# A hybrid transformer block on one core: second sequence's local attention in the rotary part's buffers, and four smaller edits

## Chip, core and metric

The kernel runs on one core of a Trainium2 chip. The metric is device time in microseconds of one execution; lower is better. "PE" is TensorE, "DVE" VectorE, "ACT" ScalarE, "POOL" GpSimd and "SP" SyncE.

## What is computed

The input `x` holds 16 sequences of 512 tokens and 256 channels, all in fp32. Four residual stages follow each other; each normalizes its input (layer norm without weights) and adds its result to `x`:

```python
x = x + _L0_attn_a_ref(_layernorm(x), Wq, bq, Wk, bk, Wv, bv, Wo, bo)   # local attention, 16 heads of 16
x = x + _L0_ffn_ref(_layernorm(x), w_gate, w_up, w_down)                # silu(gate) * up, hidden 768
x = x + _L0_attn_b_ref(_layernorm(x), Wqkv, Wout, bout)                 # rotary attention, 16 heads of 16
x = x + _L0_ffn_ref(_layernorm(x), w_gate, w_up, w_down)                # the same weights again
```

Stage a masks the scores: a token sees its 32 neighbours on either side, and the first four tokens see and are seen by all. Stage b is unusual: its numerator is `exp` of the scores of rotated queries and keys under a causal mask, while its denominator is the sum of `exp` of the unrotated scores over all keys. The feed-forward weights are integers times 1/127.

## The kernel before

One sequence is the unit of work: 512 tokens are four tiles of 128. The stages are called `a`, `f`, `b` and `h` in names and lines (`psc_gf` is a gate product of the first feed-forward part, `psc_gh` of the second). Every stage is a Python generator that yields operations with an estimated cost, the results it needs and the buffers it takes. A planner, `Plan.run`, simulates the five engines with these estimates at build time, chooses the operation that could start first on its engine, and emits it; the order in which instructions stand on each engine is the order in which the planner emitted them. So cost estimates (`LAG`, `BORDER`), the wanted distances between stages (`LEAD`, in sequences) and the numbers of buffers (`Plan({...})`) decide the order. On the chip each engine runs its list in order and waits on semaphores.

PE works in three forms, which the planner calls `lying`: the full array (`FULL`); four row strips of 32, one per head pair, for scores (`ROWS`: `sa` L664, `dn` L1097, `nm` L1157); and four column strips, for values (`COLS`: `ya` L834, `yb` L1217, `og` L929, `gq` L884). It has eight PSUM banks; a row-strip block takes four of them.

The steps of a sequence, with the names that the profile shows:

- Layer norm (`normalize`): per tile `bn_stats` and `bn_aggr` (L419, L420), then `rstd` on POOL (L424, L425), four subtract-and-multiply on DVE (`xn`, L429), transposes on PE (`lt_a`, `lt_f`, `lt_b`, `lt_h`, L457), and copies to `xnt` on DVE (L465) and ACT (L467). All of it begins when the last tile of the stage before is added.
- Local attention: `psc_ka` and `psc_qa` (L537), `psv_a` (L515), key and query copies, and splits of the queries by head parity (`split_heads`, L552: a product with a mask of one number per partition). Scores `sa`, mask added on DVE (L694), then for each half of the heads: maximum (L707, DVE), subtraction (L709, POOL), exponential (L716, ACT), sum (L718, DVE), product with the reciprocal (L724, POOL). The result is transposed (`tp`, L778), copied (`pt`, L783 on DVE and L785 on ACT), and multiplied with values (`ya`, L834) in two pieces per tile, each waiting for two of the four `pt`. Values shifted by half a block (`vw`) come by DMA from `va`. The four global tokens go their own way (`sgp`, `gq`, `tg`, `og`, `pgp`, L849). `project_out` (L491, `po_a`) ends a tile and DVE adds it to `x` (L497).
- Feed-forward: six pairs `psc_g*`, `psc_u*`, tanh on ACT (L959), two products on DVE (L961, L967), and `po_f` or `po_h`.
- Rotary attention: `psc_qb`, `psc_kb`, `psv_b`; the denominators' scores `dn` with 64 exponentials that sum (L1078); rotated scores `nm` with exponentials into a buffer `ptb` (two of them) and a causal select on POOL (L1133), values `yb`, reciprocals transposed (`dbp`, L1186), and `po_b`.

The local part's queries, keys and values of one sequence are in single buffers (`qa`, `kp`, `va`, behind the locks "a" and "va"), the rotary part's in `qb`, `qr`, `kt`, `kr` and `vb` (locks "b", "br" and "vb"). Stages of different sequences run beside each other: while sequence n is in `b`, sequence n+1 or n+2 is in `a`. At the start there is only sequence 0, at the end only sequence 15.

Of the kernel before, what the change touches and what calls it, by code (L numbers as in the profile page):

```python
# [15 lines left out]
P = 128  # L16
S = 512
# [38 lines left out]

# [9 lines left out]

def pe(us, *needs, **how):
    return Op("pe", us, *needs, **how)

# [4 lines left out]

def dve(n, *needs, us=0.0, **how):
    return Op("dve", us or 0.07 + 0.00105 * n, *needs, **how)

# [4 lines left out]

LAG = {"pe": 0.26, "act": 0.17, "dve": 0.17, "pool": 0.15, "sp": 0.1}
BORDER = 0.2
NEVER = 1e9


class Plan:
# [3 lines left out]
    def __init__(self, slots):  # L92
        self.free = dict.fromkeys(LAG, 0.0)
        self.at = {}
        self.slots = {tag: [0.0] * n for tag, n in slots.items()}
        self.threads = []
        self.lying = FULL
        self.done = {}
# [42 lines left out]

    def run(self):
        while True:
# [17 lines left out]
            if engine == "pe":  # L161
# [4 lines left out]
                        self.lying != FULL and c[1][1].lying != self.lying,  # L166
                        self.progress(c[1]),
                    ),
                )
            else:  # L170
                start, t = min(soon, key=lambda c: (not c[1][1].gives, c[1][4], c[0]))
            op = t[1]
            us = op.us
            if engine == "pe":
                if op.lying != self.lying:
                    us += BORDER
                self.lying = op.lying
                key = t[2], t[3]
# [13 lines left out]
LEAD = {"a": 0.0, "f": 0.962, "b": 2.002, "h": 2.847}  # L192
SHARE = {"a": 44.0, "f": 33.0, "b": 66.0, "h": 33.0}


@with_exitstack
def kernel(
# [108 lines left out]
    kp = const.tile([P, NC, KP], F32, tag="kp", name="kp")  # L306
    mask3 = const.tile([P, 3, P], F32, tag="mask3", name="mask3")
    sign = const.tile([P, 1], F32, tag="sign", name="sign")

    def zeros():  # L310

        yield pool(0, us=0.6, makes="zeros")
        nc.gpsimd.memset(kp[:, :, 0:HALF], 0.0)
        nc.gpsimd.memset(kp[:, :, HALF + S :], 0.0)
# [3 lines left out]
        nc.gpsimd.memset(va[:, :, :, 1, :], 0.0)  # L318

# [16 lines left out]
        yield pool(0, 30.0, us=0.5, makes="zeros_b")  # L336
        nc.gpsimd.memset(vb[:, :, :, 1, :], 0.0)
# [14 lines left out]
    def values_bias():  # L352
# [3 lines left out]
        for kc in range(NC):  # L356
# [20 lines left out]
            "pt": 3,  # L377
# [31 lines left out]
    def normalize(stage, b):  # L409

        me = f"{stage}{b}"
        needs = added(before[stage], b) if stage in before else [f"x{b}"]
        slot = input_of[stage]
        op = yield dve(0, *needs, us=1.8, takes=("xn", slot))
        xt = xs[b]
        stats = work.tile([P, NT, 6], F32, tag="stats", name=f"stats_{me}")
        mv = work.tile([P, NT, 2], F32, tag="mv", name=f"mv_{me}")
        for t in range(NT):
            nc.vector.bn_stats(stats[:, t, :], xt[:, t, :])  # L419
            nc.vector.bn_aggr(mv[:, t, :], stats[:, t, :])  # L420
        k_xn, k_in = op.k["xn"], op.k[slot]
        op = yield pool(0, op.end, us=1.3)
        rstd = work.tile([P, NT], F32, tag="rstd", name=f"rstd_{me}")
        nc.gpsimd.tensor_scalar(rstd, mv[:, :, 1], EPS, None, ALU.add)  # L424
        nc.gpsimd.tensor_tensor(rstd, rstd, neg_half, ALU.pow)  # L425
        op = yield dve(0, op.end, us=1.35)
# [48 lines left out]
        "a": ["wa", "zeros", "zeros_a"],  # L475
# [74 lines left out]
    def split_heads(dst, src, oc, par):  # L550

        nc.vector.tensor_scalar(dst[:, par, oc, :], src, par_mask[:, par : par + 1], None, ALU.mult)  # L552

    def window_attention(b):
# [4 lines left out]

        tiles = {}  # L560
# [3 lines left out]
        def query(ps, oc, k, at):  # L564
# [5 lines left out]
            for par in range(2):  # L570
                op = yield dve(0, op.end - 0.17 if par else op.end, us=0.4)
# [3 lines left out]
        for oc in range(NC):  # L575
            op = yield pe(1.72, *fed(me), takes=("u",) if oc else ("u", "a"))
            if oc == 0:
                tiles["qa"] = work.tile([P, 2, NC, S], F32, tag="qa", name=f"qa_{b}")
            ps = channels(op, xnt[me], wk_sb, oc * P, f"ka{b}_{oc}")

            def key(_, oc=oc, ps=ps):
                nc.scalar.activation(
                    kp[:, oc, HALF : HALF + S], ps, AF.Identity, bias=bqk_sb[:, 1, oc : oc + 1]
# [7 lines left out]
        yield from values("a", b, va, wv_sb, 0, "va", (("in_a", 0),))  # L591

        def copies():
            op = yield Op("sp", 0.3, *(f"v_{me}.{t}" for t in range(NT)), takes=("vw",))
            nc.sync.dma_start(vw[0][HALF:P], va[0 : P - HALF])
            nc.sync.dma_start(vw[0][0:HALF, 1:NT], va[P - HALF : P, 0 : NT - 1])
            nc.sync.dma_start(vw[1][0 : P - HALF], va[HALF:P])
            nc.sync.dma_start(vw[1][P - HALF : P, 0 : NT - 1], va[0:HALF, 1:NT])
# [9 lines left out]
        for oc in range(NC):  # L608
            for dst, src in ((kg, kp[:, oc, HALF : HALF + NG]), (qg, q[oc][:, 0:NG])):
# [34 lines left out]
        go(global_queries(b, qg))  # L644
        go(global_values(b))
        go(weighted(b))

        for t in range(NT):
# [3 lines left out]
                f"qa_{me}.1",  # L652
# [728 lines left out]
```

## Time and profile before

| what | us |
|---|---|
| median of 3 runs | 2685.93 (2683.07 to 2686.07) |
| the profiled execution | 2689.26 |
| its span, first to last instruction | 2687.5 |
| PE busy | 2610.2 (97%) |
| DVE busy | 1573.4 (59%) |
| ACT busy | 1461.5 (54%) |
| POOL busy | 958.3 (36%) |
| mean granted PE clock | 0.988 |

A profiled execution records every instruction with its start and end. "Busy" is the time in which at least one instruction of an engine ran; matmuls are pipelined, and their ends are modelled, so a busy PE need not be at its peak. A line of the page or of an answer names the source line, the engine, the operation, `out<-in`, the count, and then busy and mean times or the idle time before it with what ended it. The clock is the share of full speed that PE was granted.

### The profile page before, as it was taken

What the parts mean: (1) busy time and instruction counts of PE and PEld (TensorE: products, weight loads), DVE (VectorE), ACT (ScalarE), POOL (GpSimd) and SP (SyncE); (2) the same over time, 40 slices, a digit from 0 to 9 for tenths busy, and PEclk for the clock granted to TensorE, in tenths of its full rate; (3) what the DMA queues carried; (4) which work ended last, traced back from release to release, by engine and by line L of the source; (5) the groups of instructions that cost most, each with busy time, mean ns of one, the idle gap of its engine ahead of it and who ended that gap; (6) DMA issues with size and microseconds to landing.
All of it is one profiled execution on the core that took longest, in us unless ns stands there. A gap on an engine that the chain in (4) does not pass through costs nothing.

```text
span 2687.5 us, 55762 instructions
## 1 busy us (share of the span) xinstructions
PE 2610.2 (97%) x23396; PEld 1494.5 (56%) x23396; DVE 1573.4 (59%) x3062; ACT 1461.5 (54%) x3553; POOL 958.3 (36%) x965
## 2 busy tenths in 40 slices
PE   5899999999999999999999999999999999999997
PEld 3555556455565655656455565655656465564544
DVE  6775755566565655746566565656746566563412
ACT  2337474554746556374554746556474554746462
POOL 4543525153341523425153341523425153250301
PEclk8899999999999999999999999999999999999999
DMA  4000010000100000010000100000010000100000
GB/s 134 24 1 23 2 39 2 23 17 1 39 2 23 17 23 17 1 39 2 23 17 1 39 2 23 17 23 17 2 39 1 23 17 1 31 2 9 1 8 8
DMA packets 26586, 49.31 MB, mean 18 GB/s; under 512 B 2336, under 2 KB 21216, under 8 KB 26336
## 3 DMA queue, kind: packets, MB, share of 16 engines
q1 hardware_dynamic: 24976, 44.83, 5.8%
q8 instruction: 183, 3.00, 0.5%
q10 hardware_dynamic: 1360, 0.93, 0.1%
q14 instruction: 67, 0.55, 0.1%
HBM read 13.77 MB, written 8.39 MB: 8 GB/s over the span
## 4 chain that ended last, share of the span: by engine, by line
PE 88%; DVE 9%; POOL 2%; ACT 1%; issue 1%; DMA 0%; ACTq 0%; POOLq 0%; DVEq 0%
PE dn L1097 10%; PE po_h L491 7%; PE psc_gh L537 7%; PE psc_gf L537 6%; PE psc_uh L537 6%; PE nm L1157 6%; PE psc_uf L537 6%; PE po_f L491 6%; PE yb L1217 6%; PE tp L778 4%; PE sa L664 3%; PE psv_b L515 2%; PE psv_a L515 2%; PE ya L834 2%; PE psc_ka L537 2%; PE po_b L491 2%
## 5 line engine op out<-in xcount | busy, mean ns | idle before, releaser
L1078 ACT ACTIVATE dn<-dn 128x512 f32<-128x512 f32 x1024 | 597.1, 583 | 132.4 <-PE dn L1097 129.5
L1124 ACT ACTIVATE ptb<-nm 128x512 f32<-128x512 f32 x640 | 330.2, 604 | 230.4 <-PE nm L1157 230.0
L709 POOL TENSOR_TENSOR sc<-sc,sm 128x1056 f32<-128x1056 f32 x128 | 247.2, 1952 | 333.1 <-DVE sm L707 326.9
L1097 PE MATMUL dn<-kt,qb 32*128 32x512 f32 x2048 | 287.5, 636 | 0.0
L724 POOL TENSOR_TENSOR sc<-sc,sm 128x1056 f32<-128x1056 f32 x128 | 248.3, 1955 | 101.0 <-DVE sm L719 87.6
L1133 POOL TENSOR_SCALAR_AFFINE_SELECT ptb<-ptb 128x512 f32<-128x512 f32 x256 | 159.2, 642 | 301.5 <-ACT ptb L1124 301.5
L694 DVE TENSOR_TENSOR sc<-sa,mask 128x512 f32<-128x512 f32 x256 | 160.1, 683 | 77.9 <-PE sa L664 76.8
L537 PE MATMUL psc_gh<-xnt_h,wg_sb 128*128 128x512 f32 x384 | 186.2, 607 | 7.4 <-DVE xnt_h L465 7.3
L1157 PE MATMUL nm<-qr,kr 32*128 32x512 f32 (+3 forms) x2048 | 191.0, 465 | 0.3 <-ACT ptb L1124 0.3
L1078 ACT ACTIVATION_READ_ACCUMULATOR dn<-dn 128x1 f32 x1024 | 191.0, 187 | 0.0
L537 PE MATMUL psc_gf<-xnt_f,wg_sb 128*128 128x512 f32 x384 | 186.2, 608 | 0.6 <-DVE xnt_f L465 0.6
L537 PE MATMUL psc_uh<-xnt_h,wu_sb 128*128 128x512 f32 x384 | 185.1, 604 | 0.0
L537 PE MATMUL psc_uf<-xnt_f,wu_sb 128*128 128x512 f32 x384 | 183.6, 601 | 0.0
L718 DVE TENSOR_REDUCE sm<-sc 128x8 f32<-128x1056 f32 x128 | 158.5, 1238 | 41.2 <-ACT sc L716 41.0
L491 PE MATMUL po_h<-wd_sb,ht_h 128*128 128x256 f32 x768 | 182.0, 387 | 0.0
L491 PE MATMUL po_f<-wd_sb,ht_f 128*128 128x256 f32 x768 | 177.5, 381 | 0.6 <-ACT ptb L1124 0.5
L1217 PE MATMUL yb<-ptb,vb 128*32 128x512 f32 (+3 forms) x2048 | 168.0, 444 | 6.6 <-POOL ptb L1133 6.6
L491 PEld LDWEIGHTS po_h<-wd_sb,ht_h 128*128 128x128 f32 x768 | 141.0, 190 | 55.1 <-issue 12.6
L716 ACT ACTIVATE sc<-sc 128x1056 f32<-128x1056 f32 x128 | 136.5, 1092 | 58.5 <-POOL sc L709 58.5
L424 POOL TENSOR_SCALAR rstd_f<-mv_f 128x4 f32<-128x4 f32 x16 | 3.7, 230 | 456.1 <-DVE mv_f L420 456.1
L1097 PEld LDWEIGHTS dn<-kt,qb 32*128 32x128 f32 x2048 | 90.0, 184 | 119.4 <-issue 56.2
L707 DVE TENSOR_REDUCE sm<-sc 128x8 f32<-128x1056 f32 x128 | 155.1, 1241 | 0.0
(163 smaller groups left out, 4254.6 us busy)
## 6 DMA issues: line engine op xcount, KB each, us to landing
vw<-va SPq DMA_DIRECT2D x32, 576.0 KB, 5.7
x<-in_x_dram SPq DMA_DIRECT2D x16, 512.0 KB, 4.0
out_dram<-x SPq DMA_DIRECT2D x16, 512.0 KB, 2.9
vw<-va SPq DMA_DIRECT2D x32, 144.0 KB, 5.1
raw_wg_sb<-in_w_gate_dram SPq DMA_DIRECT2D x1, 768.0 KB, 9.7
raw_wu_sb<-in_w_up_dram SPq DMA_DIRECT2D x1, 768.0 KB, 11.1
raw_wd_sb<-in_w_down_dram SPq DMA_DIRECT2D x1, 768.0 KB, 10.9
wqkv_sb<-in_wqkv_dram SPq DMA_DIRECT2D x1, 768.0 KB, 11.6
```

The lines of the kernel that those rows point to most:

```text
L491: nc.tensor.matmul(po[:, :D], y_of(c), w_sb[:, c, :], start=(c == 0), stop=(c == n - 1))
L537: nc.tensor.matmul(ps, w_sb[:, kc, lo : lo + P], x_in[:, kc, :], start=(kc == 0), stop=(kc == NC - 1))
L694: nc.vector.tensor_tensor(flat[:, 4 * j : 4 * j + 4, 0:P], ps[j].rearrange("p c two w -> p (c two) w"), mask.unsqueeze(1).to_broadcast([P, ...
L709: nc.gpsimd.tensor_tensor(part, part, small[:, 0, hs].unsqueeze(2).to_broadcast([P, H // 2, P + NG]), ALU.add,)
L718: nc.vector.tensor_reduce(small[:, 1, hs], part, AX.X, ALU.add)
L724: nc.gpsimd.tensor_tensor(part, part, small[:, 1, hs].unsqueeze(2).to_broadcast([P, H // 2, P + NG]), ALU.mult,)
L1078: nc.scalar.activation(ps[j], ps[j], AF.Exp, scale=SCALE, accum_out=den[:, t, h : h + 1])
L1097: nc.tensor.matmul(ps[j], tiles["qb"][rows, par, oc, t * P : (t + 1) * P], tiles["kt"][rows, oc, :], start=True, stop=True,)
L1124: nc.scalar.activation(pt[:, j, :], ps[j], AF.Exp, scale=SCALE)
L1133: nc.gpsimd.affine_select(out=pt[:, :, at : at + P], in_=pt[:, :, at : at + P], pattern=[[0, 4], [1, P]], compare_op=ALU.is_ge, fill=0.0, ...
L1157: nc.tensor.matmul(ps[j][:, at : at + n], tiles["kr"][rows, oc, c * P : (c + 1) * P], tiles["qr"][rows, par, oc, c * P :], start=True, sto ...
L1217: nc.tensor.matmul(y_ps[rows, c * P :], vb[:, c, 4 * oc + j, par : par + 2, :], pt[:, j, at : at + n], start=len(seen) == 1, stop=len(seen ...
```

## The change

1. Sequence 1's local attention no longer waits for sequence 0's buffers: it takes `qb` for its split queries, a tile in the place of `qr` for its keys (`kp_2`), and `vb` for its values, and starts as a thread of its own beside sequence 0. Its scores still come after sequence 0's. `vb`'s zeros are written early for that.
2. Layer-norm statistics are made per tile, each as soon as its tile is added; `stats`, `mv` and `rstd` have a buffer per stage.
3. `split_heads` becomes a product of two tensors, with the mask broadcast along the row.
4. The values `ya` of a tile are one piece that waits for all four `pt`; `pt` has four buffers for three.
5. In the last two sequences every other exponential tile of `nm` takes a buffer of the local part's scores (`sc`) instead of `ptb`.
6. The planner's estimates change: `LAG`, `BORDER`, `LEAD`, the choice among PE operations (a price `TURN` for another form, where form came before progress), the choice on the other engines (by progress), a slow stretch of PE after a pause of over 1.5 us, and single costs. `tg` now also waits for `vw`.

The matmuls are the same in number and shape, and so are the DMAs. The core of the diff:

```diff
-LAG = {"pe": 0.26, "act": 0.17, "dve": 0.17, "pool": 0.15, "sp": 0.1}
-BORDER = 0.2
+LAG = {"pe": 0.26, "act": 0.2, "dve": 0.2, "pool": 0.2, "sp": 0.1}
+BORDER = 0.19
...
+    def turn(self, lying):
+
+        if lying == self.lying:
+            return 0.0
+        return TURN["out"] if self.lying == FULL else TURN["in"] if lying == FULL else TURN["mid"]
...
                         c[1][4],
-                        self.lying != FULL and c[1][1].lying != self.lying,
-                        self.progress(c[1]),
+                        self.progress(c[1]) + self.turn(c[1][1].lying),
...
-                start, t = min(soon, key=lambda c: (not c[1][1].gives, c[1][4], c[0]))
+                start, t = min(soon, key=lambda c: (not c[1][1].gives, c[1][4], self.progress(c[1])))
...
+                if start - self.free[engine] > 1.5:
+                    self.slow = start + 4.2
+                if start < self.slow:
+                    us += min(us, (self.slow - start) / 2)
...
-LEAD = {"a": 0.0, "f": 0.962, "b": 2.002, "h": 2.847}
+TURN = {"out": 0.15, "mid": 0.02, "in": 0.3}
+LEAD = {"a": 0.0, "f": 0.796, "b": 1.467, "h": 2.654}
...
+    kp_2 = work.tile([P, NC, KP], F32, tag="qr", name="kp_2")
...
-            "pt": 3,
+            "pt": 4,
...
-        op = yield dve(0, *needs, us=1.8, takes=("xn", slot))
-        xt = xs[b]
-        stats = work.tile([P, NT, 6], F32, tag="stats", name=f"stats_{me}")
-        mv = work.tile([P, NT, 2], F32, tag="mv", name=f"mv_{me}")
         for t in range(NT):
+            op = yield dve(0, needs[t], us=0.51)
+            if t == 0:
+                xt = xs[b]
+                stats = work.tile([P, NT, 6], F32, tag=f"stats_{stage}", name=f"stats_{me}")
+                mv = work.tile([P, NT, 2], F32, tag=f"mv_{stage}", name=f"mv_{me}")
             nc.vector.bn_stats(stats[:, t, :], xt[:, t, :])
             nc.vector.bn_aggr(mv[:, t, :], stats[:, t, :])
...
-        nc.vector.tensor_scalar(dst[:, par, oc, :], src, par_mask[:, par : par + 1], None, ALU.mult)
+        mask = par_mask[:, par : par + 1].to_broadcast([P, S])
+        nc.vector.tensor_tensor(dst[:, par, oc, :], src, mask, ALU.mult)
...
+        second = b == 1
+        keys, v_all, locks, v_lock = (kp_2, vb, ("b", "br"), "vb") if second else (kp, va, ("a",), "va")
...
+                f"scored_a{b - 1}",
                 takes=("s", "sc", "small"),
-                gives=(("a", 0),) if t == NT - 1 else (),
+                makes=f"scored_{me}" if t == NT - 1 else None,
+                gives=[(lock, 0) for lock in locks] if t == NT - 1 else (),
...
-            for ns in ((0, 1), (2, 3)):
+            for ns in (range(4),):
...
-        op = yield pe(0.4, op.end, takes=("u",), gives=(("tmp", k_gp),))
+        op = yield pe(0.4, op.end, f"vw_{me}", takes=("u",), gives=(("tmp", k_gp),))
...
+        def home(i):
+
+            return "sc" if b >= B - 2 and i % 2 else "ptb"
...
-        plan.start(in_turn(bodies[stage], stage), stage, 0)
+        if stage == "a":
+            plan.start(bodies[stage](0), stage, 0)
+            plan.start(in_turn(bodies[stage], stage, 0, 1), stage, 1)
+        else:
+            plan.start(in_turn(bodies[stage], stage), stage, 0)
```

## The prediction

> **What bounds the kernel now.** I read the page first: its busy times, its 40 slices, and the chain that ended last.
>
> ```profile
> PE 2610.2 (97%) x23396; PEld 1494.5 (56%) x23396; DVE 1573.4 (59%) x3062; ACT 1461.5 (54%) x3553; POOL 958.3 (36%) x965
> ...
> PE   5899999999999999999999999999999999999997
> ...
> PEclk8899999999999999999999999999999999999999
> ...
> PE 88%; DVE 9%; POOL 2%; ACT 1%; issue 1%; DMA 0%; ACTq 0%; POOLq 0%; DVEq 0%
> ```
>
> TensorE (PE) works nearly all the time; only the first and last slices have holes. Next, busy time by stage (columns: width, then busy us of PE, PEld, DVE, ACT, POOL, then the granted clock):
>
> ```profile
> 0.00:60.00 60.00, 32.18 (x447) 21.93 (x447) 36.21 (x69) 12.39 (x18) 27.83 (x40) 0.83 0.48 150
> 60.00:120.00 60.00, 48.05 (x589) 31.18 (x587) 54.31 (x100) 19.38 (x31) 36.48 (x33) 0.89 0.10 26
> 120.00:300.00 180.00, 174.57 (x1874) 103.15 (x1876) 120.12 (x220) 97.34 (x230) 77.48 (x70) 0.97 0.04 10
> 300.00:2400.00 2100.00, 2088.16 (x19112) 1201.05 (x19105) 1261.32 (x2470) 1187.17 (x2892) 772.27 (x771) 1.00 0.06 17
> 2400.00:2600.00 200.00, 195.35 (x998) 99.64 (x997) 83.84 (x169) 112.67 (x311) 32.04 (x35) 0.99 0.01 4
> 2600.00:2687.50 87.50, 71.90 (x400) 37.55 (x392) 17.63 (x36) 32.51 (x73) 12.16 (x19) 0.90 0.04 13
> ```
>
> PE is idle 27.8 + 12.0 + 5.4 us in the first 300 us, 11.8 us in the next 2100, 20.3 us after that. The granted clock is below 1 only at the two ends; there PE is slow as well as idle. PE's waits name the holes:
>
> ```profile
> PE tg L909 <- DVE gp L905: 13.9, 1, 13.9
> PE lt_a L457 <- DVE xn_a L429: 10.1, 2, 9.5
> PE lt_f L457 <- DVE xn_f L429: 9.3, 4, 6.9
> PE lt_h L457 <- DVE xn_h L429: 8.6, 4, 4.6
> PE psc_gh L537 <- DVE xnt_h L465: 7.3, 13, 0.8
> PE yb L1217 <- POOL ptb L1133: 6.6, 6, 1.9
> ```
>
> The first four are sequence 0's softmax, the first load, and layer norms; all but the fifth lie mostly in the ramps. A busy PE is not at its best either. The timeline late in the run (start, length) shows it:
>
> ```profile
> 2500.87 1.15 PE L1157 MATMUL nm<-qr,kr 32*128 32x384 f32 x16
> 2501.95 1.07 PE L1217 MATMUL yb<-ptb,vb 128*32 128x384 f32 x16
> 2502.95 2.86 PE L491 MATMUL po_f<-wd_sb,ht_f 128*128 128x256 f32 x12
> 2505.74 1.15 PE L1157 MATMUL nm<-qr,kr 32*128 32x256 f32 x16
> ```
>
> From start to start, `nm` costs 1.08 us, `yb` 1.00, `po_f` 2.79. Alone, 512 columns in two passes take 0.858 us (a `psc` pair repeats every 1.717), so these stream in 0.858, 0.858 and 2.573. The rest, 0.22, 0.14 and 0.21, is the price of going from one form of tile (row strips, column strips, full array) to another. With that the profiled span divides: 9.5 us to the first matmul; 2313.6 of streaming (144.6 a sequence); 247.8 of turns between blocks; 4.7 after the last matmul; and 111.9 of waits and slow clock, namely 55.9 before 300 us, 20.9 from 300 to 2400, 35.1 after. The change leaves the matmuls alone, so it can act on the turns and on the 111.9.
>
> **Turns.** I counted neighbours in the order of instructions of both programs and priced them by the mean of the same kind in this trace, waits left out. Leaving row strips costs 0.22, full to row 0.153, column to full 0.143, column to row 0.124, full to column 0.108, full to full 0.049. Row to full goes 294 to 277, row to column 117 to 174, full to row 324 to 397, column to full 135 to 167, column to row 87 to 54, full to column 105 to 47, full to full 1059 to 1044; the few others hardly move. One value piece per tile does halve the runs of `ya` (128 to 64), but the planner's new rule for turns lets `dn` stand in 247 runs where it stood in 217. The sum goes from 247.8 to 253.7: **+6 us** (+2 to +10, since some neighbours are new).
>
> **Start.** `tg` waits for sequence 0's global softmax while DVE and POOL work down the local one:
>
> ```profile
> 35.91 1.64 PE L457 MATMUL lt_a<-ident,xn_a 128*128 128x128 f32 x8 [0.58 <-DVE xn_a L429]
> 51.44 0.68 PE L909 MATMUL tg<-ident,gp 64*128 64x64 f32 x4 [13.89 <-DVE gp L905]
> ```
>
> In the new order sequence 1's `psc_ka`, `psc_qa`, `psv_a` (4 x 1.72 + 4 x 0.9 = 10.5 us) stand in this hole; before, they filled PE between 69 and 90 us. Sequence 0's chain hardly changes. Eight mask adds at 0.62 a piece and four maxima at 1.19 end on DVE at 45.6 (46.8 before), then three subtractions and two products on POOL at 1.95 make tile 0 ready at 51.8, and `tp` starts at 52 where it started at 54.4. Now the price: those fillers are gone later. By the same durations PE waits about 4 us after the projections, 2.5 for `ya`, 1.3 for `yag`, 4.7 before the third tile's `tp` (DVE also has sequence 1's four splits), 2.5 for `pgp`, 1 for the fourth `tp` and 6 for `lt_f0`, whose layer norm gains 1.6 us as three of its four statistics (0.53 each) are made early. That puts `psc_gf0` at 104.5 instead of 110.5. With PE's own work before it (61.2 us of streaming and turns, 60.5 before), 40.5 us of waits become 33.8. After it, sequence 1 is further on, and `lt_f1` has 5.7 us of PE work between its last `po_a` and itself; the 9 us lost there before (2.9 idle, and 184.7 to 191.5 at a clock of 0.50) should fall to 3. Against this, more pauses keep the clock low: the pause of about 2.7 us at 183 was followed by that stretch of half clock, the 13.9 us one by half clock from 38 to 58. Five pauses of 2.5 to 6 us at 0 to 2 us each, little where PE waits anyway: I take 1. Together 6.7 + 6.3 - 1: 55.9 becomes 44, **-12** (-20 to -4).
>
> [...]
>
> **Splits.** 192 instructions change form.
>
> ```profile
> L552 DVE TENSOR_SCALAR qa<-q,masks x64: 435/486/2170, 23.1 to 2277.6; 128x512 f32<-128x512 f32 x64
> ...
> L694 DVE TENSOR_TENSOR sc<-sa,mask x256: 671/681/693, 33.0 to 2382.6; 128x512 f32<-128x512 f32 x128
> ```
>
> The old form takes 0.48 alone but up to 2.17 beside POOL (at 76.0 two took 3.85 us while a POOL product ran). Products of two SBUF tensors (L1009, L1011) took 0.69 alone and at most 1.26. Old busy sum: 110.8 us. New: 192 x 0.62 to 0.69 = 119 to 132 us. DVE is busy 60% of the middle, so this is hidden at **0**; without that cover it would be 1.3 us a sequence. [...]
>
> **Middle.** A sequence takes 161.1 us here: 144.6 of streaming, 15.3 of turns, 1.2 of waits (`lt_h` behind `xn_h`, `psc_gh` behind `xnt_h`). Leads and lags change the order, so I compared the PE work between producer and consumer with the time from the one to the other in this trace. Last `po_b` to `lt_h`: 8.0 us of work becomes 10.3, the chain takes 8.0. `nm` to `yb`: 3.0 becomes 4.1, for 2.0 to 4.8. `tp` to `ya`: 1.7 becomes 2.2, for 0.7. Last `po_f` to `lt_b`: 8.6 becomes 7.0, for 7.5 less 1.6 of early statistics. `dn` to the next user of its banks: 2.1 becomes 2.0, for 1.9. Only `lt_h` to `psc_gh` shrinks to the bone: 3.1 becomes 1.9, for a copy of 0.69 and whatever DVE has queued. I take 0.5 us a sequence where there were 1.2, beside some 5 us in the first two sequences: 20.9 becomes 12, **-9** (-15 to +20).
>
> **Tail.** `lt_h14` cost about 5 us (2.6 idle, then 3.4 at half clock); it now has 7.7 us of `po_f` work ahead of it. The last rotary part, from `nm_15` at 2602.8 to `po_b15` at 2638.6, waits for two exponential buffers; with `sc` as a second pair ACT can run through: twelve exponentials at 0.6 from 2599.7, forty at 0.51, two copies, then 3.7 us of select, `yb` and product end at 2632 to 2636. The last layer norm saves 1.6. **-12** (-15 to -3).
>
> Vector memsets, DMA orders and the fourth `pt` buffer cost nothing: POOL is idle 1.5 us before the first `rstd`, and the counts of DMAs are equal.
>
> **Sum.** -12 - 9 - 12 + 6 = -27 us. The profiled execution took 2689.26 (span 2687.5 and 1.8 around it), 3.3 above the median of the runs. So 2662 for such an execution, and 2685.9 - 27 = **2659** as a median.
>
> **Rivals.** *The start only moves its waits* (0.20): DVE is busy 54.3 of 60 us from 60 to 120, more than PE, and gets sequence 1's work earlier; the 12 us are not won, 2671. For it: the five new pauses. Against: the hole of 13.9. *All ramps fill* (0.12): start 20 and tail 15, 2646 or less. *DVE becomes the bound between layer norm and `psc_gh`* (0.07), slower: splits and per-tile statistics queue ahead of the `xnt_h` copy, and PE has 1.9 us of cover where it had 3.1. Each us late is 16 us; it eats the 27 at 1.7 us a sequence, and at 2.5 the time is 2699. Against: the copy is ranked first, and DVE has 40% free. *The order brings nothing* (0.06): the turns and new waits pay back what the ramps give, 2685.
>
> **Chances.** Forecast 0.55 (2650 to 2668). The measurement can tell about 0.2%, 5.4 us. Forecast, filled ramps and moved waits are faster: 0.87; nothing 0.06; slower 0.07. The range runs from -45 (start 20, middle 15, tail 15, turns +5) to -3 (start 4, tail 7, middle +2, turns +6): 2641 to 2683.
>
> **What would show it.** Right: no `tg` wait of 13.9; `psc_gf0` near 104 to 108; a spacing of 160.9 to 161.5 us between sequences; `po_b15` to the end unchanged but for 1.6 us; turns up. Wrong: `psc_gh <- xnt_h` above 1 us on every sequence; `psc_gf0` at 110 or later; splits above 1 us in the mean.

## The result, and the profile after

The changed kernel took 2718.86 us (median of 5 runs, 2717.86 to 2729.53), beside 2685.93 (2680.71 to 2686.8, 5 runs) for the kernel before on the same chip: a ratio of 1.014, 95% interval 1.0117 to 1.0163. (Further on, brackets behind a time hold the same two: the ratio to the kernel before and its interval.) It is 33 us slower where 27 us faster were forecast. The profiled execution took 2718.34 (span 2716.6).

The page of after, its busy times and its chain that ended last:

```profile
PE 2622.4 (97%) x23396; PEld 1492.2 (55%) x23396; DVE 1659.2 (61%) x3062; ACT 1456.5 (54%) x3553; POOL 1010.6 (37%) x967
...
PE 81%; DVE 17%; POOL 1%; issue 1%; DMA 1%; ACT 0%; ACTq 0%; SPq 0%; POOLq 0%; DVEq 0%
```

DVE has as many instructions as before and 86 us more work; its share of the chain went from 9% to 17%. Busy time by stage, after (columns as in the prediction):

```profile
0.00:60.00 60.00, 40.97 (x344) 26.84 (x352) 44.67 (x92) 15.75 (x24) 32.21 (x45) 0.94 0.50 150
60.00:120.00 60.00, 45.40 (x734) 31.32 (x716) 53.61 (x91) 17.70 (x28) 40.28 (x36) 0.89 0.10 26
...
300.00:2400.00 2100.00, 2059.08 (x18484) 1160.74 (x18488) 1300.19 (x2408) 1161.31 (x2854) 791.28 (x744) 1.00 0.06 17
```

The hole of the first 60 us is smaller (PE busy 41.0 where it was 32.2). In the middle, from 300 to 2400 us, PE is idle 40.9 us where it was 11.8. The clock is nearly full there: it was granted at half for two stretches of 6.8 us (from 316.3 and from 1804.5), where in before it never was. PE's waits in after (total us, times, longest):

```profile
PE dn L1111 <- DVE pt L797: 18.1, 12, 1.8
PE tp L792 <- DVE vb L533: 16.9, 12, 1.5
PE lt_a L464 <- DVE xn_a L436: 14.5, 4, 9.5
PE pgp L820 <- POOL pq L814: 7.4, 5, 4.4
PE lt_f L464 <- DVE xn_f L436: 6.4, 2, 5.0
PE lt_h L464 <- DVE xn_h L436: 4.5, 2, 3.6
```

The 13.9 us of `tg` are gone, and `lt_f` and `lt_h` wait less, as expected. The first two rows are new: 12 sequences, each 1.5 us for `dn` and 1.4 for `tp`. The releasers are plain copies of 0.4 to 0.7 us, so the question is what DVE did ahead of them. The timeline of one sequence (start, length; DVE, then POOL, then PE) answers it:

```profile
1621.05 3.32 DVE L560 TENSOR_TENSOR qb<-tmpb,masks 128x512 f32<-128x512 f32 x2
...
1629.57 2.10 DVE L1023 TENSOR_TENSOR tmpb<-tmpb,sins 128x512 f32<-128x512 f32 x1
...
1632.38 0.42 DVE L533 COPY vb<-psv_b 128x256 f32<-128x256 f32 x1
1632.72 3.09 DVE L560 TENSOR_TENSOR qr<-tmpb,masks 128x512 f32<-128x512 f32 x2
...
1637.73 0.68 DVE L797 COPY pt<-tp 128x512 f32<-128x512 f32 x1
...
1619.52 4.30 POOL L723 TENSOR_TENSOR sc<-sc,sm 128x1056 f32<-128x1056 f32 x2 [4.35 <-DVE sm L721]
1626.55 4.58 POOL L738 TENSOR_TENSOR sc<-sc,sm 128x1056 f32<-128x1056 f32 x2 [1.04 <-DVE sm L733]
1631.85 1.74 POOL L1017 TENSOR_TENSOR kr<-kt,cos 128x512 f32<-128x512 f32 x1
1633.56 1.71 POOL L1017 TENSOR_TENSOR tmpb<-tmpb,cos 128x512 f32<-128x512 f32 x1
...
1632.86 1.09 PE L792 MATMUL tp<-ident,sc 128*128 128x128 f32 x8 [1.46 <-DVE vb L533]
1638.46 1.14 PE L1111 MATMUL dn<-kt,qb 32*128 32x512 f32 x8 [1.82 <-DVE pt L797]
```

Two `qb` splits take 3.32 us while POOL's softmax products of the next sequence run; a sine product takes 2.10 beside the second pair; then come `vb`, two `qr` splits of 3.09 beside POOL's cosine products, and `pt`. PE waits for `vb` and for `pt`. The groups of DVE in after (busy, mean ns) show the splits' price:

```profile
L560 DVE TENSOR_TENSOR qb<-tmpb,masks 128x512 f32<-128x512 f32 x64 | 80.9, 1284 | 1.7 <-ACT tmpb L1032 1.7
L560 DVE TENSOR_TENSOR qr<-tmpb,masks 128x512 f32<-128x512 f32 x64 | 63.3, 1008 | 0.1
L560 DVE TENSOR_TENSOR qa<-q,masks 128x512 f32<-128x512 f32 x64 | 44.1, 729 | 114.2 <-ACT q L579 114.2
```

In before the same groups, in the old form, were these:

```profile
L552 DVE TENSOR_SCALAR qa<-q,masks 128x512 f32<-128x512 f32 x64 | 47.1, 773 | 32.4 <-ACT q L568 32.4
L552 DVE TENSOR_SCALAR qb<-tmpb,masks 128x512 f32<-128x512 f32 x64 | 32.5, 541 | 10.1 <-ACT tmpb L1018 10.1
L552 DVE TENSOR_SCALAR qr<-tmpb,masks 128x512 f32<-128x512 f32 x64 | 31.2, 511 | 0.9
```

From here on "splits" is count times mean over the 192: 116.8 us before, 193.3 after. (The prediction's 110.8 is busy time, which counts overlapping instructions once.)

The table divides every profiled span as the prediction did: streaming is taken as 2313.6 us in all of them, turns are counted from the order at the prediction's prices, waits are what is left by stage, so they hold what a lower clock costs as well.

| kernel | us, median | turns | waits to 300 | 300 to 2400 | later | DVE busy | splits |
|---|---|---|---|---|---|---|---|
| before | 2685.93 | 247.8 | 55.9 | 20.9 | 35.1 | 1573 | 117 |
| after | 2718.86 | 253.4 | 52.3 | 58.9 | 24.3 | 1659 | 193 |
| splits_back | 2687.71 | 253.4 | 51.0 | 30.7 | 22.5 | 1617 | 151 |
| splits_alone | 2699.70 | 247.8 | 53.9 | 31.3 | 40.0 | 1609 | 155 |
| old_rules | 2674.81 | 242.6 | 57.5 | 20.7 | 23.5 | 1627 | 169 |
| old_rules_ts | 2658.84 | 243.5 | 53.8 | 12.9 | 19.7 | 1581 | 122 |
| pool_narrow | 2651.18 | 253.4 | 37.3 | 8.9 | 21.2 | 1576 | 149 |
| pool_busy | 2653.80 | 253.4 | 40.8 | 9.5 | 21.5 | 1595 | 153 |

### The profile page after: what moved, and what is told of

It is laid out like the page before. It is cut to its first block, busy times and chain, and to the rows that moved or that the text cites. A ratio compares the mean times of both kernels' runs of the same rounds, so it can differ in the third digit from the quotient of the medians.

```text
span 2716.6 us, 55822 instructions
## 1 busy us (share of the span) xinstructions
PE 2622.4 (97%) x23396; PEld 1492.2 (55%) x23396; DVE 1659.2 (61%) x3062; ACT 1456.5 (54%) x3553; POOL 1010.6 (37%) x967
## 4 chain that ended last, share of the span: by engine, by line
PE 81%; DVE 17%; POOL 1%; issue 1%; DMA 1%; ACT 0%; ACTq 0%; SPq 0%; POOLq 0%; DVEq 0%
PE dn L1111 9%; PE po_h L498 7%; PE psc_gf L544 6%; PE nm L1176 6%; PE psc_uf L544 6%; PE po_f L498 6%; PE yb L1236 6%; PE psc_uh L544 6%; PE psc_gh L544 5%; PE tp L792 3%; DVE qb L560 3%; PE psv_a L522 2%; PE po_b L498 2%; PE sa L678 2%; PE psc_qa L544 2%; PE ya L848 2%
## 5 line engine op out<-in xcount | busy, mean ns | idle before, releaser
L723 POOL TENSOR_TENSOR sc<-sc,sm 128x1056 f32<-128x1056 f32 x128 | 253.3, 1998 | 213.6 <-DVE sm L721 211.9
L1111 PE MATMUL dn<-kt,qb 32*128 32x512 f32 x2048 | 305.0, 640 | 21.0 <-DVE pt L797 18.1
L738 POOL TENSOR_TENSOR sc<-sc,sm 128x1056 f32<-128x1056 f32 x128 | 258.0, 2029 | 59.2 <-DVE sm L733 57.8
L708 DVE TENSOR_TENSOR sc<-sa,mask 128x512 f32<-128x512 f32 x256 | 160.9, 682 | 51.3 <-PE sa L678 51.3
L1176 PE MATMUL nm<-qr,kr 32*128 32x384 f32 (+3 forms) x2048 | 188.8, 464 | 0.9 <-issue 0.9
L732 DVE TENSOR_REDUCE sm<-sc 128x8 f32<-128x1056 f32 x128 | 157.7, 1232 | 37.3 <-ACT sc L730 37.3
L498 PEld LDWEIGHTS po_h<-wd_sb,ht_h 128*128 128x128 f32 x768 | 141.0, 190 | 41.8 <-ACT dn L1092 13.9
L792 PE MATMUL tp<-ident,sc 128*128 128x128 f32 x1024 | 142.5, 288 | 21.7 <-DVE vb L533 16.9
L975 DVE SCALAR_TENSOR_TENSOR th_f<-th_f,psc_gf 128x512 f32<-128x512 f32 x96 | 65.3, 680 | 150.0 <-ACT th_f L973 149.4
## 6 DMA issues: line engine op xcount, KB each, us to landing
raw_wu_sb<-in_w_up_dram SPq DMA_DIRECT2D x1, 768.0 KB, 10.3
```

Of the source, the lines that this page charges most:

```text
L498: nc.tensor.matmul(po[:, :D], y_of(c), w_sb[:, c, :], start=(c == 0), stop=(c == n - 1))
L708: nc.vector.tensor_tensor(flat[:, 4 * j : 4 * j + 4, 0:P], ps[j].rearrange("p c two w -> p (c two) w"), mask.unsqueeze(1).to_broadcast([P, ...
L723: nc.gpsimd.tensor_tensor(part, part, small[:, 0, hs].unsqueeze(2).to_broadcast([P, H // 2, P + NG]), ALU.add,)
L738: nc.gpsimd.tensor_tensor(part, part, small[:, 1, hs].unsqueeze(2).to_broadcast([P, H // 2, P + NG]), ALU.mult,)
L792: nc.tensor.transpose(ps[:, j, :], sc[:, j, oc, par, 0:P], ident)
L1111: nc.tensor.matmul(ps[j], tiles["qb"][rows, par, oc, t * P : (t + 1) * P], tiles["kt"][rows, oc, :], start=True, stop=True,)
```

## Experiments 1: the form of the split, or the order

**Theory FORM**: the tensor product (edit 3) stalls beside POOL, VectorE comes late, PE waits. **Rival ORDER**: the planner's new rules (edit 6) put the work there, whatever its form. Two runs change the form alone, two the rules. "Rules" are `LAG`, `BORDER`, `LEAD`, `TURN`, both choices and the slow stretch.

```diff
 # splits_back: after, one instruction
-        nc.vector.tensor_tensor(dst[:, par, oc, :], src, mask, ALU.mult)
+        nc.vector.tensor_scalar(dst[:, par, oc, :], src, par_mask[:, par : par + 1], None, ALU.mult)
```

> The kernel after, with the split into heads as a product with a per-partition scalar again; the order of instructions on every engine is that of after. Theory FORM (the tensor product with a broadcast mask reads two SBUF tensors and stalls beside POOL's products, so VectorE comes late with the copies vb and pt): the splits fall from 193 us of VectorE to about 120, PE's waits from 300 to 2400 us fall from 59 to 15 to 25, time 2675 to 2690. Theory ORDER (the planner's new leads, lags and choice put VectorE's rotary work beside POOL's softmax products and the consumers close behind; the form of the split hardly matters, since the old form stalls beside POOL as well): the waits stay at 45 to 59, time 2705 to 2719.

Measured 2687.71 (ratio to before 1.0009, 1.0000 to 1.0019): 31 us of the 33 are gone, in the same order of instructions. The waits of the middle halve. But the splits fall only to 151 us. Its groups show that the old form is slow in these places too:

```profile
L559 DVE TENSOR_SCALAR qb<-tmpb,masks 128x512 f32<-128x512 f32 x64 | 65.0, 1037 | 1.7 <-ACT tmpb L1031 1.7
L559 DVE TENSOR_SCALAR qr<-tmpb,masks 128x512 f32<-128x512 f32 x64 | 48.7, 781 | 0.1
```

The form costs 1284 - 1037 = 0.25, 0.23 and 0.19 us, about the difference of the two alone (0.68 and 0.48). The stall on top is nearly the same (`qb` 0.60 us in the tensor product and 0.56 in the old form, `qr` 0.33 and 0.30): FORM was right in time (its waits of 15 to 25 were 30.7) and wrong in mechanism.

```diff
 # splits_alone: before, one instruction
-        nc.vector.tensor_scalar(dst[:, par, oc, :], src, par_mask[:, par : par + 1], None, ALU.mult)
+        mask = par_mask[:, par : par + 1].to_broadcast([P, S])
+        nc.vector.tensor_tensor(dst[:, par, oc, :], src, mask, ALU.mult)
```

> The kernel before, with the split into heads as a tensor product and nothing else; the order of instructions is that of before. FORM: VectorE's time in the splits rises from 111 to 170 or more, PE's waits in the middle from 21 to 45 or more, time 2710 to 2725. ORDER: the splits cost 0.2 us more each (192 of them, 35 to 40 us of VectorE), hidden by its idle 40 per cent; time 2683 to 2692.

Measured 2699.70 (1.0053, 1.0038 to 1.0068), between the two. The splits cost 38 us more of VectorE, 0.2 each, and 14 of them reach the end. `lt_h <- xn_h` (8.6 to 12.7) and `psc_gh <- xnt_h` (7.3 to 11.5), waits that were there before, grow by 8 of the 14. The 155 us also answer the prediction's bound of 119 to 132: it fails in the old order already.

> The kernel after, with the planner's lags, leads, price of a turn, rule of choice and clock model of before. Counted from the order and priced as in the prediction, its turns cost 242.6 us where after has 253.4. FORM: the tensor products stay, VectorE's splits stay above 160 us, and only the turns are won: 2700 to 2712. ORDER: the waits of the middle go as well: 2655 to 2680.

Measured 2674.81 (0.9958, 0.9942 to 0.9975): faster than before, with the tensor product. Turns fall and the new waits of the middle go, as ORDER said, though the splits still cost 169 us, as FORM said.

> The kernel before, with only the planner's new lags, leads, price of a turn, rule of choice and clock model. Turns by count 257.7 us (before 247.8). FORM: the old form of the split keeps VectorE in time; only the turns are lost, less something at the ends: 2685 to 2698. ORDER: the waits of the middle come with the rules, 40 us or more: 2715 to 2735.

Measured 2829.05 (1.0533, 1.0517 to 1.0548), far beyond both: the middle waits 137 us, with the clock at half for 116.1 us of it; `dn` waits 32.5 for `vb`, in an order where the old form of `qb` takes 1.28 us in the mean.

> The kernel after, with the planner's rules of before and the split as a product with a scalar (cost in the plan 0.4 again): the second sequence's place, the statistics by tile, the one value piece and the second exponential pair remain. Its turns are 243.5 us by count. If the tensor product costs in this order what it cost in that of before (14 us): 2658 to 2664. If an order that keeps it from POOL makes it free: 2671 to 2678. With the start or tail worth nothing: 2680 or more.

Measured 2658.84 (0.9906, 0.9891 to 0.9921), 0.94% or some 25 us faster than before, and no kernel with the whole computation was faster. Of the three cases it is the first (2658 to 2664). So, with edits 1, 2, 4 and 5 in all four:

| | old form of split | tensor product |
|---|---|---|
| rules of before | 2658.84 | 2674.81 |
| new rules | 2687.71 | 2718.86 |

The form costs 16 or 31 us, the rules 29 or 44: each costs more beside the other, as when both take slack from one engine. (In the upper row the planned cost of a split changes with the form, so a few instructions move too.)

## Experiments 2: is it POOL that VectorE waits for

Every DVE instruction of 300 to 2400 us in the trace of after, sorted by the POOL instruction that overlaps it most, gives these means: `qb` 1.29 us beside the softmax products (49 of 52); `qr` 0.67 alone and 1.34 and 1.75 beside the cosine products; the sine product 0.68 alone, 2.10 beside a softmax product. But `sc <- sa,mask`, which reads PSUM, 0.68 alone and 0.69 beside one, and the maximum over `sc`, which reads one SBUF tensor, 1.24 and 1.24. `xn_h`, a tensor_scalar that also reads one, takes 0.40 alone and 1.80 beside a softmax product. So of these the products of two SBUF tensors and tensor_scalar lose time (0.6 to 1.4 us beside a softmax product), and the mask add, which reads PSUM, and the maximum do not. The loss looks like a block: the two `qb` splits of the timeline above end 0.55 us behind the second softmax product (1624.37 and 1623.82).

Three runs test whether the time is lost there.

```diff
 # pool_narrow: after, both POOL products of the local softmax (the other one likewise)
-                part,
-                part,
-                small[:, 0, hs].unsqueeze(2).to_broadcast([P, H // 2, P + NG]),
+                part[:, 0:1],
+                part[:, 0:1],
+                small[:, 0, hs.start : hs.start + 1].unsqueeze(2).to_broadcast([P, 1, P + NG]),
 # pool_busy: the same, and after each product
+            nc.gpsimd.memset(part[:, 2:], 0.0)
+            nc.gpsimd.memset(part[:, 2:], 0.0)
```

> The kernel after in its own order, but POOL's two products of the local softmax (add of the maximum, product with the reciprocal) are done on one head of eight in each half: 132 columns of 1056, so POOL is free 1.7 us earlier each time. It leaves out the shift and the normalization of the other seven heads. Theory SHARE (the tensor product on VectorE is slow because it runs while POOL's product runs): qb falls from 1.28 to about 0.70 us in the mean, qr, whose neighbour is POOL's product with cos, stays at 0.9 or more, the wait of tp for vb goes, time 2680 to 2700. Rival FORM IN ITSELF (in this order the tensor product is slow for another reason, such as ScalarE writing beside it): qb stays above 1.1 us, time 2705 to 2719.

> The kernel after in its own order; POOL's two products of the local softmax are done on one head of eight, as in pool_narrow (2651 us), and POOL then writes zeros over the last six heads twice, so that it is busy about 2.0 us as in after but for three quarters of that time reads nothing from SBUF. It leaves out the shift and the normalization of the other heads. Theory STALL (the loss is VectorE's stall beside POOL's products of two SBUF tensors): VectorE is free again, splits qb 0.75 to 0.90 us in the mean, time 2650 to 2670, near pool_narrow. Rival LATENCY (pool_narrow was fast because each step of the softmax chain came 1.6 us earlier, and the copies behind it with it): time 2700 to 2719, near after, although the splits are short. Rival WRITES (any work of POOL in SBUF stalls VectorE): qb stays above 1.1 us.

pool_narrow measured 2651.18 (0.9879, 0.9863 to 0.9895), better than either theory said, and pool_busy 2653.80 (0.9889, 0.9872 to 0.9905). In pool_busy POOL is as long at each step as in after, as its groups show:

```profile
L747 POOL MEMSET sc<- 128x792 f32 x128 | 97.4, 761 | 7.4
...
L746 POOL MEMSET sc<- 128x792 f32 x128 | 97.1, 759 | 0.0
...
L740 POOL TENSOR_TENSOR sc<-sc,sm 128x132 f32<-128x132 f32 x128 | 59.5, 465 | 39.6 <-DVE sm L735 38.0 <-DVE sc L702 0.2
```

and in after:

```profile
L738 POOL TENSOR_TENSOR sc<-sc,sm 128x1056 f32<-128x1056 f32 x128 | 258.0, 2029 | 59.2 <-DVE sm L733 57.8 <-ACT th_f L973 0.2 <-DVE sc L702 0.2
```

0.47 + 0.76 + 0.76 = 1.98 us, where the whole product took 2.03. Yet the time falls by 65 us, as much as DVE's busy time (1659.2 to 1594.7). For the splits LATENCY and WRITES fall; STALL stands. Beside the zeros `qb` takes 0.73 in the mean, beside the products of after 1.29. The splits `qb` and the middle of pool_busy:

```profile
L560 DVE TENSOR_TENSOR qb<-tmpb,masks 128x512 f32<-128x512 f32 x64 | 48.5, 778 | 1.8 <-ACT tmpb L1036 1.7
...
300.00:2400.00 2100.00, 2099.21 (x19072) 1189.76 (x19075) 1284.49 (x2474) 1180.99 (x2889) 781.34 (x1181) 1.00 0.06 17
```

PE is idle 0.8 us of 2100. In the order of after, with the tensor products and with POOL as busy, hardly anything is late once DVE does not stall beside the softmax products. The splits are not all of it: they sum to 153 us here and to 151 in splits_back, which is 34 us slower. The stalled sine product (2.10 to 0.70) and `xn_h` (1.80 to 0.92) are cured here too, and not there.

```diff
 # qb_psum: after; the bank is given back behind the second split
-                split_heads(tiles["qb"], qt, oc, par)
+                split_heads(tiles["qb"], ps, oc, par)
```

> The kernel after, with the split of the unrotated query reading the projection's PSUM bank instead of ScalarE's copy of it in SBUF; the bank is given back after the second split instead of after the copy, so the plan moves a little (turns by count 250.5 us, after 253.4), and the splits qb still stand between softmax reductions of the next sequence, beside POOL's 2 us products. Theory SHARE (only instructions of VectorE that read SBUF alone, as two tensors or as one in the fast form, stall beside a POOL product of two SBUF tensors; in the trace of after the products with a PSUM operand keep 0.68 us beside it): qb falls from 1.28 to 0.66 to 0.70 us, VectorE gets back 35 to 40 us, and the time falls to 2685 to 2705. Rival FORM IN ITSELF (slow beside anything): qb stays above 1 us. Rival BANK (the bank comes free later and PE waits for it): qb 0.68, time 2715 or more.

("The fast form" is the product with a scalar, read from SBUF: 0.48 us alone where the tensor product takes 0.68.)

```profile
L560 DVE TENSOR_TENSOR qb<-psc_qb,masks 128x512 f32<-128x512 f32 x64 | 40.3, 671 | 3.0 <-ACT tmpb L1032 3.0
```

The split is cured: 0.67 us in the mean where after has 1.28, and 46 of 52 still stand beside POOL's softmax products. The time falls by 10 us only: 2708.79 (1.0085, 1.0070 to 1.0100), 4 us above the range. The middle:

```profile
300.00:2400.00 2100.00, 2081.09 (x18517) 1174.48 (x18519) 1267.07 (x2413) 1168.13 (x2861) 773.99 (x748) 0.99 0.06 17
```

PE is idle 18.9 us there where after has 40.9, but the clock was granted at half for 30.7 us where after has 13.7. `dn` still waits 7.7 us for `pt` and 4.8 for `vb`. The plan moved, and now one `xn_b` of each sequence meets POOL's product (1.49 us in the mean, 0.40 alone). So the operand's place cures this instruction (1.28 to 0.67 us); what the kernel wins by that alone is not shown, since order and clock changed with it.

> The kernel of old_rules_ts (2659) with the split of the unrotated query reading PSUM, as in qb_psum. Its turns are 243.5 us by count, as there. The splits qb cost 0.64 us in the mean there, so little is to be won: STALL gives 10 us of VectorE less and 2653 to 2660. If the later release of the bank or the moved order costs more: 2665 or more.

Measured 2658.91 (0.9910, 0.9895 to 0.9924), equal to old_rules_ts. It does not tell what the stall of `qb` is worth in that order: the scalar form takes 0.74 us from PSUM, alone and beside POOL's cosine products, where it took 0.64 in the mean from SBUF, so DVE got no time back (busy 1580.0 us, 1581.2 in old_rules_ts).

## Experiments 3: which rule

```diff
 # leads_old: after, one line
-LEAD = {"a": 0.0, "f": 0.796, "b": 1.467, "h": 2.654}
+LEAD = {"a": 0.0, "f": 0.962, "b": 2.002, "h": 2.847}
```

> The kernel after, with one line of the planner back: LEAD of before (a 0, f 0.962, b 2.002, h 2.847). In its order the splits qb and qr of a sequence stand behind the next sequence's last pt copies, no longer among its softmax reductions; by count its turns cost 238.4 us (after 253.4). Theory PLACE (the new leads put VectorE's rotary products beside POOL's 2 us softmax products): the mean split falls from 1.0 to about 0.69 us, the waits of the middle from 59 to 15 to 25, time 2658 to 2678. Rival CLOSE (the new choice of PE's next step and the lags put consumers close behind producers, whatever the leads): the waits stay above 40 and only the turns are won, 2698 to 2710.

Measured 2716.84 (1.0123, 1.0108 to 1.0138): neither. PLACE is half right on the splits (`qb` and `qr` at a median of 0.68 us, but a mean of 0.87 over all splits, since part of them meet POOL's products) and wrong on the time. Turns fall by 15 us by count. PE waits 29.9 us for `xn_a`, of which 15.2 are in the middle, where after has none. The timeline of leads_old (DVE, POOL, PE):

```profile
1266.03 4.46 DVE L436 TENSOR_SCALAR xn_a<-x,mv_a,rstd_a 128x256 f32<-128x256 f32 x4
...
1265.43 1.95 POOL L723 TENSOR_TENSOR sc<-sc,sm 128x1056 f32<-128x1056 f32 x1
...
1267.99 1.98 POOL L723 TENSOR_TENSOR sc<-sc,sm 128x1056 f32<-128x1056 f32 x1
...
1270.18 1.69 PE L464 MATMUL lt_a<-ident,xn_a 128*128 128x128 f32 x6 [1.62 <-DVE xn_a L436]
```

Four `xn_a`, 0.40 us each alone, take 4.46 between two softmax products: the same stall, another victim, and PE waits for it 11 times in the middle.

Then one rule at a time, added to old_rules_ts. (The slow stretch after a pause was not tried alone.)

> The kernel of old_rules_ts (2659) with one line more of the change: the new LEAD. Turns by count 257.1 us (243.5), and the splits qb, qr stand ahead of the copies vb and pt of the next sequence again, beside POOL's softmax products. Theory LEADS (this line carries what the planner's rules lose beside the splits' form): 14 us of turns and 10 to 20 of waits, time 2678 to 2692. Rival OTHER RULES (the loss comes with the choice of PE's next step and the lags): turns alone at most, 2660 to 2674.

Measured 2742.18 (1.0218, 1.0200 to 1.0236), beyond LEADS. `dn <- vb` 15.9 us and `lt_h <- xn_h` 15.3; waits of the middle 84.3, turns 257.1. DVE is busy only 5 us more than in old_rules_ts (1586.2 and 1581.2) while the kernel is 83 us slower, so more stalled time on DVE in total is not the cause here. Whether it is the place of the stalls or the order itself stays open; the clock was granted at half for 44.4 us of the middle (old_rules_ts 3.4).

> The kernel of old_rules_ts with the new price of a turn in PE's choice (progress plus price, where before a step of another form stood behind in any case), leads of before. Turns by count 230.2 us (243.5): 13 us less. If the waits stay as in old_rules_ts: 2644 to 2650. Rival (each new order brings its own collisions with POOL's products, as the new leads with the old rest and the old leads with the new rest did): 2660 to 2690, with a wait of the layer norms or of the copies above 10 us in the middle.

Measured 2801.50 (1.0444, 1.0428 to 1.0459). It has the cheapest turns of all, 230.2, and is the slowest but one. PE's waits in x_turn:

```profile
PE tp L786 <- POOL sc L732: 23.4, 16, 4.7
PE lt_b L459 <- DVE xn_b L431: 22.8, 24, 1.7
PE lt_a L459 <- DVE xn_a L431: 20.1, 23, 9.5
```

The rival named them and was too small: 140 us of waits in the middle, and from one `lt_b` to the next now 131, now 210 us.

> The kernel of old_rules_ts with the new LAG and BORDER alone (lags of ACT, DVE and POOL 0.2 where they were 0.17, 0.17, 0.15). Turns by count 248.8 us (243.5). If lags only shift the order: 2660 to 2668. If they bring consumers too close behind producers or splits beside POOL: 2675 or more.

> The kernel of old_rules_ts with the new choice on the other engines alone (among steps of equal rank the one whose stage is furthest behind, not the one ready first). Turns by count 242.8 us (243.5). If this choice only reorders equal steps: 2655 to 2663. If it makes VectorE late with the copies that PE waits for: 2670 or more.

Measured 2686.83 (1.0013, 1.0004 to 1.0022) and 2685.04 (1.0006, 0.9996 to 1.0015). Lags longer by 0.03 to 0.05 us, or another choice among equal steps, cost 26 to 28 us. In x_choice `psc_qb <- xnt_b` waits 10.3 us. So no single rule carries the loss: old_rules_ts lies well among its neighbours, and each of the four rules tried alone leads away from it. That these losses are the stall is not shown. For after, pool_busy shows it; for leads_old the timeline shows it for `xn_a`, which is 15 of the 34 us that PE is idle in the middle.

## Experiments 4: what the other edits are worth

Each run undoes one edit in old_rules_ts.

> The kernel of old_rules_ts without the second sequence's place in the rotary part's buffers (one set of keys, queries and values for the local attention, as before). FILLED (the second sequence's projections fill the wait for the first global softmax, as forecast, 12 us): 8 to 14 us slower than old_rules_ts, with tg's wait of 13.9 back. MOVED (the waits come back in the next hundred us): within 4 us of it.

2661.88 (0.9916, 0.9901 to 0.9930), MOVED: 3 us slower than old_rules_ts, with overlapping intervals. A wait of 13.8 us is back, before `tp` and not before `tg`. To 60 us PE is idle 28.0 us where old_rules_ts has 19.8, from 60 to 120 it is 10.9 where that has 14.2.

> The kernel of old_rules_ts with the statistics of a layer norm in one piece, as before. Turns by count 240.0 us (old_rules_ts 243.5). If the statistics by tile shorten the waits for the layer norms as forecast (1.6 us for each that PE waits for, in the first two sequences and the tail, and some in the middle): 2662 to 2672. If not: 2653 to 2660, by the turns.

2697.60 (1.0043, 1.0028 to 1.0058): statistics by tile are worth 39 us here, three times the most expected. Without them `lt_b` and `lt_h` wait 12.9 and 12.4 us (4.8 and 4.5 in old_rules_ts); `xn_b` meets POOL's softmax products there 13 times at 1.9 us.

> The kernel of old_rules_ts with the values of the local attention in two pieces per tile and three pt buffers, as before. Turns by count 250.0 us (old_rules_ts 243.5), so 2663 to 2668 if the pieces matter by the turns alone; 2656 to 2661 if waits for the fourth transposed piece pay that back.

2675.07 (0.9973, 0.9958 to 0.9988): 16 us, more than expected, of which 6.5 are turns and 8 are waits spread over the stages.

> The kernel of old_rules_ts without the second pair of exponential buffers for the last two sequences. Turns equal by count. If the last rotary part waits for two buffers as read from the trace of before (after 2600 us): 6 to 12 us slower, 2665 to 2671, all of it after 2550 us. If the order has already taken that wait away: within 3 us of old_rules_ts.

2666.67 (0.9931, 0.9916 to 0.9946): 8 us, all in the tail (waits after 2400 us 30.1, old_rules_ts 19.7).

## Why the prediction failed, step by step

- **Turns**: 253.4 where 253.7 was forecast. That confirms the order and not the prices, since both are counted at the prices of before. The neighbours that the prediction lists make +13.5 at its prices; for its +6 the others must lose 7.6, so "hardly move" is wrong (column to column goes from 70 to 28).
- **Tail**, right: waits after 2400 us 35.1 to 24.3, -10.8 where -12 was forecast; the second pair of buffers is worth 8 in the order of old_rules_ts (x_no_home).
- **Start**, mis-sized: -3.6 where -12 was forecast. The filling is there (PE idle 27.8 to 19.0 us in the first 60), and 60 to 300 us gave back half of it (17.4 to 22.0), above all in `pgp <- pq` (6.5) and `tp`. `psc_gf0` came at 107.9, in the range given for it and not at the 104.5 of the sum. The 6.3 us taken for `lt_f1` were misadded: 6.8 us at half clock lose 3.4, so the loss at 183 was 6.3 and not 9, with 3 of it to remain. `lt_f1` itself does wait only 1.4 us now, yet from 120 to 300 us PE is idle 7.4 us where it was 5.4. The "pause of about 2.7 us" there is three gaps of 0.48, 0.94 and 0.94 between transposes, and the half clock begins at 184.7, within the third, so that row shows no single pause of 2.7 us. The step as a whole is the rival "the start only moves its waits", by its mechanism. With DVE freed of the stall (pool_busy) these 300 us wait 40.8, which is -15: here too the durations were taken without their new neighbours.
- **Splits**, the step that failed: "DVE is busy 60% of the middle, so this is hidden at 0". The instructions were bounded at 119 to 132 us by rows in the order of before. In that order they cost 155 (splits_alone): the new form stalls just as the old one does (`qa` takes 0.98 us in the mean and 0.68 alone, in the old form 0.77 and 0.48), and its 0.2 us come on top, 38 us in all where 119 to 132, beside 110.8, left 8 to 21. In the new order they cost 193, because it puts them beside POOL's products. And the cover was an average. Where PE waits for a copy behind them there was none: of 42.5 us of DVE that the form costs, 31 reach the end.
- **Middle**, which that step carries: -9 forecast, +38 measured, beyond even the +20 of its own bounds, of which the range took only +2. From one `lt_b` to the next mostly 164 to 165 us pass where 160.9 to 161.5 were to show the forecast right. The distances between producers and consumers were enough: with the same order and no stall beside the softmax products the waits are 9.5 where the prediction put 12. But the durations put against them were those of before, each with its old neighbour. The prediction listed the producers and never asked what POOL would run meanwhile, though its own row of 2.17 us for a split beside a POOL product had shown the price.
- **Rivals**: "DVE becomes the bound" was the right mechanism at 0.07, at the wrong place: `psc_gh <- xnt_h` was feared, and `dn <- pt`, `tp <- vb` came. Of its signs of being wrong, splits above 1 us in the mean came true (1.007).
- **Sum**: -27 us is, by luck, about what edits 1, 2, 4 and 5 bring without edits 3 and 6, but by other terms: old_rules_ts, at 2658.84 where 2659 was forecast for the whole change, has turns -4, start -2, middle -8 and tail -15.

## What to carry to other kernels

An instruction's price is its duration beside what will run next to it, not beside what ran there before: the same split took 0.68 us alone and 1.29 in the mean beside a GpSimd product of 2.0 us. When a change moves work on VectorE, list for each instruction what GpSimd does at the same moment, and price products of two SBUF tensors and tensor_scalar from SBUF at their stalled time there (here 1.29 for 0.68 us, and 1.80 for 0.40). "60% busy" is no cover for an instruction with a copy queued behind it that TensorE waits for: here it waited 35.0 us for `pt` and `vb`. And constants of a planner are fitted to an order: each of four rules taken singly cost 26 to 143 us here, whatever the count of turns said.

## What was not expected of the hardware

- A 128x512 fp32 product of two SBUF tensors on VectorE: 0.68 us alone, 0.73 beside GpSimd's memset, 1.29 in the mean and 2.43 at most beside a GpSimd product of 2.0 us (after). With one operand in PSUM: 0.67 beside the same product (qb_psum).
- A 128x256 tensor_scalar from SBUF (`xn`): 0.40 us alone, 0.44 beside GpSimd's copy, 0.72 beside its affine select (before), 0.91 beside its memset (pool_busy), 1.80 beside its product (after). So beside the memset it takes 0.51 us more than alone, the product of two SBUF tensors 0.05 more.
- GpSimd pays less: the 79 softmax products of after that overlap a split, a sine product or an `xn` take 2.16 us in the mean and 2.40 at most, the other 177 take 1.95.
